# Half of a 7x7 depthwise convolution in steps between the layers of an MLP, and waits for reused memory by tile

## The chip, the cores and the metric

The kernel runs on one core of one Trainium2 chip. The metric is the device time of one execution in microseconds (us). Three executions of the kernel before took 5678.27, 5685.37 and 5686.59 us, and their median is 5685.37 us.

## What is computed

The input `x` has 8 images of 96x96 positions with 192 channels, all in float32. Two residual blocks follow one another. `_gn` is a group normalisation with 32 groups of 6 channels over a whole image.

```python
def block_0(x, W_in, b_in, conv_w, ln_g, ln_b, W_out, b_out):
    proj = einsum('bhwd,dc->bhwc', x, W_in) + b_in
    local = depthwise_conv_3x3(proj, conv_w)
    lr, rl, tb, bt = ema_scans_in_four_directions(local)
    mixed = 0.25 * (lr + rl + tb + bt) + local
    return einsum('bhwc,cd->bhwd', layer_norm(mixed) * ln_g + ln_b, W_out) + b_out

def block_1(x, dw_kernel, dw_bias, ln_gamma, ln_beta, w0, b0, w1, b1, gamma):
    y = depthwise_conv_7x7(x, dw_kernel) + dw_bias
    y = layer_norm(y) * ln_gamma + ln_beta
    y = gelu(einsum('bhwc,cd->bhwd', y, w0) + b0)
    return (einsum('bhwd,dc->bhwc', y, w1) + b1) * gamma

x = x + block_0(_gn(x), ...)
x = x + block_1(_gn(x), ...)
```

Block 0 widens 192 channels to 384, block 1 widens them to 768.

## The kernel before

The work is done in five stages, one after another, and each stores its result in device memory for the next. The order of instructions within a stage is written out by hand (`manual_schedule`); each engine works through its own list in order, and so do the lists of SP and GpSimd that issue DMAs.

1. **Projection** (to 756 us of the profiled execution). Normalised columns are turned and multiplied with `W_in`; the result goes to `P_d`.
2. **3x3 convolution and scans** (to about 1795 us). Groups of four channels are convolved by banded matrices on TensorE, scanned on VectorE (lines 631 and 640), mixed, and stored to `M_d`.
3. **Residual of block 0** (to 2639 us). A loop over 192 columns of 4 images each. Every column is loaded (`mt`, `xr`), normalised, multiplied with `wc` (line 866), added to `x` (`x1c`, line 883) and stored to `X1_d` in tiles of 16 columns (`store_c`, line 982). The statistics for the second group normalisation are taken on the way (line 903). For each half of the images a chain of six small steps turns them into a scale and a shift in `s1`. The first half's chain runs in the middle of the stage. The second half's runs at its end (lines 920 to 968), ahead of the next stage.
4. **7x7 convolution** (2680 to 3247 us). There are 32 pieces: two halves of the images (4 images each) times 16 groups of 12 channels. A piece loads `raw` from `X1_d` (six DMAs, three from SP and three from GpSimd, line 773) and its `band` of banded matrices from `Z2_d` (line 777, one DMA, SP and GpSimd by turns). VectorE copies `band` to the other 64 partitions (line 1049) and scales `raw` into `xin` (line 1059, 16 instructions). Then follow six steps of `conv_d`: 12 matmuls each of 63 rows by 64 columns (line 1079; float32 makes two records of each), on four tiles of the array, and two evictions on ScalarE (line 1089) into `yo`. Six DMAs store `yo` to `Y_d` (lines 1104 to 1109). `raw`, `band`, `xin` and `yo` have two buffers each. The loads of pieces 0 and 1 are issued in stage 3, 24 and 12 columns before its end.
5. **MLP** (3247 us to the end). There are 72 units `u` of 1024 positions, 36 in each half of the images; a block `n` of two units shares one load of `y` (from `Y_d`, line 1164) and one of `r` (from `X1_d`, line 1173). Per unit, VectorE takes statistics (`stats_e`) and normalises (`norm_e`, line 1198; its power is on GpSimd, line 29), TensorE transposes (`turn_in`, line 1213), then multiplies with `w0w` (`first_layer`, lines 1230 and 1240) in two parts of six PSUM banks. ScalarE applies Gelu (line 1249), TensorE multiplies with `w1g` in four parts `k` (`second_layer`, line 1260), VectorE adds `r` into `xo` (line 1270), and GpSimd issues the store (line 1278). GpSimd also adds the bias to `r` (`bias_r`, line 1179). First layers of unit `u` stand between second layers of unit `u - 1`. All seven banks of `hp` serve both layers; one bank serves the transposes.

Pools of tiles are opened and closed by stage. A pool that takes memory of a closed pool waits, before anything is written, until every tile of the earlier pool has been released.

## Time and profile before

| | us |
|---|---|
| median of three executions | 5685.37 |
| the profiled execution | 5683.71 |
| its span | 5681.8 |
| TensorE busy in the span (94%) | 5361.7 |
| VectorE busy (53%) | 3007.6 |
| ScalarE busy (39%) | 2226.5 |
| GpSimd busy (37%) | 2091.8 |
| second-layer matmuls, line 1260: busy | 1148.7 |
| first-layer matmuls, lines 1230 and 1240: busy | 769.3 and 409.8 |
| 7x7 matmuls, line 1079: busy | 426.5 |

By stage, TensorE is busy for 706.65 of 756 us, 1021.75 of 1039, 805.46 of 844, 435.98 of 608 (2639 to 3247 us) and 2391.90 of 2435. The DMA engines have a share of 0.86, 0.91, 0.92, 0.89 and 0.31 in these stretches.

How to read the lines shown below: PE is TensorE, PEld its weight loads, DVE VectorE, ACT ScalarE, POOL GpSimd, SP the engine that issues most DMAs. In the slices of the page each digit is the busy share of one of 40 equal parts of the span, in tenths. A table of stretches gives, for each stretch from:to, its length, the busy time of each engine with its number of instructions, the clock granted to TensorE (PEclk, 1.00 is full), the share of the 16 DMA engines that was busy, and GB/s. A line of waits names who waited for whom, the total in us, how often, and the longest. A line of DMA issues gives out<-in, the issuing queue, the number, KB each and the median us to landing.

### The profile page before, as it was taken

The page shows a single profiled execution, that of the slowest core. Times are in us where ns is not written, and L with a number is a line of the kernel's source. Part 1 is how long each engine was busy: PE and PEld are TensorE (multiplying, and loading weights), DVE is VectorE, ACT ScalarE, POOL GpSimd, SP SyncE. Part 2 cuts the span into 40 slices and gives each one's busy share as a digit, 9 for nine tenths or more (in the row PEclk, how much of TensorE's full clock was granted, in tenths as well). Part 3 has the DMA queues.
Part 4 walks back from the last instruction along what each step waited for, and adds up shares of the span by engine and source line. Part 5 has one row for each costly group of instructions (what it writes and reads, how often), then busy time and mean ns, then how long its engine had stood idle before and what let it go on. Part 6 is the DMA issues. An engine that isn't in the chain of part 4 may idle for free.

```text
span 5681.8 us, 106371 instructions
## 1 busy us (share of the span) xinstructions
PE 5361.7 (94%) x43070; PEld 3424.8 (60%) x43070; DVE 3007.6 (53%) x6098; ACT 2226.5 (39%) x5282; POOL 2091.8 (37%) x2093
## 2 busy tenths in 40 slices
PE   6999989999998999997777689999999999999999
PEld 4666633333334999986333257767777676776767
DVE  6656459999997455545444343334333333333432
ACT  2444447777775666553333322222222222222221
POOL 1111148888887555553222122222222222222221
PEclk9999989999999999998888899999999999999999
DMA  7999879999997899997999833322322332332221
GB/s 222 289 289 266 227 208 242 245 244 245 243 243 214 266 288 289 279 286 203 272 262 273 230 73 76 74 69 69 79 70 68 79 71 69 72 76 70 69 69 39
DMA packets 695475, 996.57 MB, mean 175 GB/s; under 512 B 234232, under 2 KB 576809, under 8 KB 692937
## 3 DMA queue, kind: packets, MB, share of 16 engines
q1 hardware_dynamic: 598488, 620.61, 43.6%
q0 software_dynamic: 90368, 366.55, 20.1%
q8 instruction: 340, 5.57, 0.4%
q10 hardware_dynamic: 6128, 2.61, 0.2%
q14 instruction: 151, 1.23, 0.1%
HBM read 585.22 MB, written 419.93 MB: 177 GB/s over the span
## 4 chain that ended last, share of the span: by engine, by line
PE 74%; DMA 6%; issue 3%; DVE 2%; SPq 1%; POOL 1%; ACT 0%; POOLq 0%; DVEq 0%
PE po L1260 19%; PE hp L1230 12%; PE pl L598 11%; PE po L866 10%; PE hp L1240 7%; PE pa L619 5%; PE pt L864 3%; DMA band<-Z_d 3%; DMA raw<-X_d 3%; PE pa L622 2%; PE py L1079 2%; PE pt L1213 2%; DVE xin L1059 1%; SPq L773 1%; DMA mt<-M_d 1%
## 5 line engine op out<-in xcount | busy, mean ns | idle before, releaser
L1249 ACT ACTIVATE g<-hp,b0g 128x512 f32<-128x512 f32 x864 | 514.9, 695 | 1850.3 <-PE hp L1240 1850.3
L1260 PE MATMUL po<-w1g,g 128*128 128x192 f32 x6912 | 1148.7, 326 | 0.0
L1260 PEld LDWEIGHTS po<-w1g,g 128*128 128x128 f32 x6912 | 1121.6, 190 | 1.5 <-issue 1.5
L1230 PE MATMUL hp<-yT,w0w 128*128 128x512 f32 x1728 | 769.3, 595 | 0.0
L1216 DVE COPY yT<-pt 128x512 f32<-128x512 f32 x216 | 148.8, 689 | 1058.8 <-PE pt L1213 1058.8
L866 PE MATMUL po<-wc,mt 128*128 128x193 f32 x3456 | 686.7, 334 | 2.2 <-DVE x1c L883 2.2
L598 PE MATMUL pl<-pin,band 34*32 34x380 f32 (+1 forms) x13824 | 629.3, 489 | 18.5 <-DMA pin<-P_d 18.5
L671 POOL TENSOR_TENSOR mo<-mo,z 128x768 f32<-128x768 f32 x288 | 601.4, 2089 | 3.1 <-ACT mo L623 0.2
L866 PEld LDWEIGHTS po<-wc,mt 128*128 128x128 f32 x3456 | 556.3, 192 | 32.9 <-ACT mean L868 30.1
L1079 PE MATMUL py<-xin,band 63*64 63x372 f32 (+1 forms) x4608 | 426.5, 517 | 146.6 <-DVE xin L1059 146.6
L1278 POOL DMA_DIRECT2D out_dram<-xo x288 | 210.5, 731 | 893.7 <-DVE xo L1270 876.5
L1230 PEld LDWEIGHTS hp<-yT,w0w 128*128 128x128 f32 x1728 | 322.1, 191 | 347.1 <-issue 345.4
L631 DVE TENSOR_TENSOR_SCAN z<-decay,loc 128x768 f32<-128x768 f32 x288 | 505.8, 1756 | 42.1 <-ACT loc L607 13.2
L640 DVE TENSOR_TENSOR_SCAN z<-decay,z 128x768 f32<-128x768 f32 x288 | 498.3, 1730 | 0.1
L598 PEld LDWEIGHTS pl<-pin,band 34*32 34x32 f32 x13824 | 232.3, 107 | 397.6 <-issue 395.2
L619 PE MATMUL pa<-loc,mix 128*32 128x384 f32 x3456 | 431.7, 493 | 0.0
L1270 DVE TENSOR_TENSOR xo<-po,r 128x384 f32<-128x384 f32 x288 | 232.6, 808 | 369.1 <-PE po L1260 369.1
L622 PE MATMUL pa<-last,down 96*32 96x384 f32 x1152 | 426.7, 493 | 0.9 <-ACT mo L623 0.9
L1079 PEld LDWEIGHTS py<-xin,band 63*64 63x64 f32 x4608 | 184.3, 144 | 388.3 <-issue 298.6
L1240 PE MATMUL hp<-yT,w0w 64*128 64x512 f32 x1728 | 409.8, 606 | 0.0
L29 POOL TENSOR_TENSOR rs<-rs_ve,neg_half 128x8 f32<-128x8 f32 x72 | 118.9, 1651 | 778.6 <-DVE rs_ve L28 757.5
L381 PE MATMUL pm<-xT,win 128*128 128x384 f32 x1152 | 392.2, 491 | 0.0
(133 smaller groups left out, 6693.2 us busy)
## 6 DMA issues: line engine op xcount, KB each, us to landing
P_d<-po POOLq DMA_DIRECT2D x96, 1152.0 KB, 9.9
pin<-P_d SPq DMA_DIRECT2D x192, 576.0 KB
mt<-M_d SPq DMA_DIRECT2D x192, 576.0 KB
xq<-in_x_dram SPq DMA_DIRECT2D x96, 576.0 KB
xr<-in_x_dram SPq DMA_DIRECT2D x192, 288.0 KB
X_d<-x1c SPq DMA_DIRECT2D x144, 384.0 KB
y<-Y_d SPq DMA_DIRECT2D x144, 384.0 KB
r<-X_d SPq DMA_DIRECT2D x36, 1536.0 KB
```

The lines of the kernel that those rows point to most:

```text
L598: nc.tensor.matmul(pls[g][at * RB : (at + 1) * RB, :, lo:hi], band[rows, c, kh, :], pin[rows, c, :, NJ - 1 - j, lo + kh - 1 : hi + kh - 1] ...
L619: nc.tensor.matmul(pa[at], mix[:, i, at], loc[:, q], start=True, stop=True)
L622: nc.tensor.matmul(pa[at], down[:, to], last[:, q], start=True, stop=True)
L631: nc.vector.tensor_tensor_scan(zf, decay_f, loc.rearrange("p q n -> p (q n)"), 0.0, ALU.mult, ALU.add)
L640: nc.vector.tensor_tensor_scan(zr, decay_f, zr, 0.0, ALU.mult, ALU.add)
L671: nc.gpsimd.tensor_tensor(m, m, z, ALU.add)
L866: nc.tensor.matmul(po, lhs[m], wc[:, m], start=(m == 0), stop=(m == NC - 1))
L1079: nc.tensor.matmul(pys[g][k * 64 : (k + 1) * 64, :, lo:hi], band[rows, k * GS + c, d * ZS : d * ZS + 64], xin[rows, :, :, k * GS + c, lo + ...
L1230: nc.tensor.matmul(hps[m, q], w0w[:, 2 * q, m * 128 : (m + 1) * 128], yT[:, 2 * q], start=True, stop=False,)
L1240: nc.tensor.matmul(hps[m, q], w0w[p, 1, m * 128 : (m + 1) * 128], yT[p, 1], start=False, stop=True,)
L1249: nc.scalar.activation(g[:, m, q], hps[m, q], AF.Gelu, bias=b0g[:, m : m + 1], scale=1.0)
L1260: nc.tensor.matmul(po[:, q], g[:, m, q, k * 128 : (k + 1) * 128], w1g[:, m], start=(m == 0), stop=(m == NE - 1),)
```

## The change

The change has five parts.

- **Pieces in the MLP.** Only the first 18 of the 32 pieces (`N1 = NI + 2`: all of the first half of the images and two of the second) are a stage of their own. The other 14 are cut into slots: three slots of eight scalings (the third also spreads the band) and six slots of one `conv_d` step. The loads of the next `raw` are issued with the first step; the store and the load of the next band with the last. `slot()` takes the next one, at five places of each unit of the first half's MLP.
- **First half's MLP.** The first layer runs in three parts of four banks instead of two of six. Five banks (`ps_h`) serve both layers, two (`ps_y`) the steps. In the second half the seven banks are used in turn, in two parts as before. `yn` has one buffer instead of two, and `xo` three of a quarter unit instead of two of a whole one.
- **Stage 4.** Its pieces alternate between two sets of buffers (`early` and `own`); `raw` is three tiles, one for each `t`, and 24 scalings (one for each `t`, image and group) replace 16. From piece 18 on there is one set. The band of piece `n + 1` is loaded ahead of the raw of piece `n + 2`.
- **Edges.** Piece 0 is loaded 20 columns before the end of stage 3, and scaled in its last ten. The normalisation chain of the second half stands between the steps of pieces 1 and 2. The first two `y` are loaded at piece 16, and the first unit is normalised at piece 17. `X1_d` and `Y_d` are one tensor for each half.
- **Memory.** All pools from stage 2 on have `reuse_waits="tile"`: a tile waits for the tiles that had its memory, not for the whole closed pool. `avg` moves to a pool of stage 1, `ones` is dropped.

The diff, cut to its core:

```diff
-    X1_d = dram.tile([B * ROWS + 1, NGC, NV, GC * WQ], F32, name="X1_d")
-    Y_d = dram.tile([ROWS, 2, GROUPS, NH, NV, GS * WQ], F32, name="Y_d")
+    X1_d = [
+        dram.tile([NH * ROWS + 1, NGC, NV, GC * WQ], F32, name=f"X1_{hf}") for hf in range(2)
+    ]
+    Y_d = [dram.tile([ROWS, GROUPS, NH, NV, GS * WQ], F32, name=f"Y_{hf}") for hf in range(2)]
...
+    by_tile = dict(reuse_waits="tile")
-        bp_ = ph.enter_context(tc.tile_pool(name="b_in", bufs=4))
+        bp_ = ph.enter_context(tc.tile_pool(name="b_in", bufs=4, **by_tile))
...
+    early = ctx.enter_context(tc.tile_pool(name="d_early", bufs=1, **by_tile))
+    N1 = NI + 2
+    d_pools = [early, None]
+    def load_raw(n, t):
+        hf, i = todo[n]
+        pool = d_pools[0 if n == 0 or n >= N1 else (n + 1) % 2]
+        raw = pool.tile([128, NH, NV, GC, WQ], F32, tag="raw", name="raw", bufs=NT)
...
+    def load_band(n):
+        pool = d_pools[0 if n >= N1 else n % 2]
...
+        (nc.sync, nc.gpsimd)[g].dma_start(
+            band[g * 64 : (g + 1) * 64].rearrange("q c l -> q (c l)"),
+            Z2_d[:, i * GC : (i + 1) * GC].rearrange("r c l -> r (c l)"),
+        )
+    def scale_steps(n):
...
+        for t in range(NT):
+            for b in range(NH):
+                for k in range(2):
+                    steps.append(lambda t=t, k=k, b=b: scale(t, k, b))
+        return steps + [spread]
...
-                if u in (n_u - 24, n_u - 12):
-                    first_d.append(load_d(0, len(first_d)))
+                if u == n_u - 20:
+                    load_band(0)
+                    for t in range(NT):
+                        load_raw(0, t)
+                    first_d += scale_steps(0)
+                if u >= n_u - 10:
+                    for step in first_d[:3]:
+                        step()
+                    del first_d[:3]
...
+    ps_t = ctx.enter_context(tc.tile_pool(name="e_ps_t", bufs=1, space=PSUM, **by_tile))
+    ps_h = ctx.enter_context(tc.tile_pool(name="e_ps_h", bufs=5, space=PSUM, **by_tile))
+    ps_y = ctx.enter_context(tc.tile_pool(name="d_ps", bufs=2, space=PSUM, **by_tile))
+    def bank(pool=None):
+        if pool is None:
+            pool = ps_h if ring[0] % 7 < 5 else ps_y
+            ring[0] += 1
+        return pool.tile([128, 512], F32, tag="hp", name="hp")
...
+            load_band(1)
+            for t in range(NT):
+                load_raw(1, t)
+            norms = norm_c(1, bank)
+            for n in range(N1):
+                if n:
+                    store_d(n - 1)
+                    load_band(n + 1)
+                if n == NI:
+                    load_y(0)
+                    load_y(1)
+                if n == N1 - 1:
+                    for t in range(NT):
+                        load_raw(N1, t)
+                    prepare(0)
+                else:
+                    if n + 2 < N1:
+                        for t in range(NT):
+                            load_raw(n + 2, t)
+                    for step in scale_steps(n + 1):
+                        step()
+                if n == 2:
+                    make_weights(bank())
+                for c in range(GS):
+                    conv_d(n, c)
+                    if 0 < n < 3 and c % 2:
+                        norms.pop(0)()
+            store_d(N1 - 1)
...
+        for n in range(N1, len(todo)):
+            more = n + 1 < len(todo)
+            scales = scale_steps(n)
+            slots += [scales[:8], scales[8:16], scales[16:]]
+            slots += [[lambda n=n, c=c: conv_d(n, c, ps_y)] for c in range(GS)]
+            if more:
+                slots[-GS] += [lambda n=n, t=t: load_raw(n + 1, t) for t in range(NT)]
+            slots[-1].append(lambda n=n: store_d(n))
+            if more:
+                slots[-1].append(lambda n=n: load_band(n + 1))
...
+            first_layer(u, 0, parts, pool)
+            turn_in(u + 1, 0) if u < n_u else None
+            slot()
...
+            second_layer(u - 1, 0, pool)
+            slot()
+            if early_half:
+                first_layer(u, 1, parts, pool)
+            second_layer(u - 1, 1, pool)
+            turn_in(u + 1, 1) if u < n_u else None
+            slot()
...
+            if not early_half:
+                first_layer(u, 1, parts, pool)
+            turn_in(u + 1, 2) if u < n_u else None
...
+            second_layer(u - 1, 2, pool)
+            slot()
+            if early_half:
+                first_layer(u, 2, parts, pool)
...
+            second_layer(u - 1, 3, pool)
+            slot()
```

## The prediction

> **What bounds the kernel now.** I read four views of the kernel before: the page's 40 slices, the busy time by stretch, the waits of TensorE around the 7x7 stage, and the DMA issues. The slices come first:
>
> ```profile
> PE   6999989999998999997777689999999999999999
> ...
> PEclk9999989999999999998888899999999999999999
> DMA  7999879999997899997999833322322332332221
> ```
>
> TensorE is full nearly everywhere. In slices 19 to 23, where the 7x7 convolution lies, it is not: its digit is 7 or 6, its clock is down, and DMA is at 9 in slices 20 to 22. From slice 24 on DMA falls to 2 or 3 and TensorE is full. The stretches say how much:
>
> ```profile
> core 0: us, PE busy (x) PEld busy (x) DVE busy (x) ACT busy (x) POOL busy (x), PEclk, DMA share, GB/s
> 2640.00:2700.00 60.00, 27.90 (x239) 16.76 (x243) 34.07 (x82) 7.48 (x15) 11.44 (x10) 0.63 0.51 130
> 2735.00:3247.00 512.00, 385.66 (x4172) 166.63 (x4172) 214.15 (x476) 182.07 (x347) 110.12 (x179) 0.85 0.93 258
> 3250.00:3320.00 70.00, 36.11 (x100) 15.67 (x101) 36.61 (x81) 12.01 (x19) 15.73 (x5) 0.71 0.66 131
> 3320.00:5640.00 2320.00, 2320.00 (x10940) 1639.53 (x10941) 883.74 (x2216) 500.56 (x840) 498.91 (x383) 1.00 0.30 70
> ```
>
> Pieces 3 to 32 of the convolution take 512 us, 17.07 us a piece, with the DMA engines 93% busy and TensorE only 385.66/30 = 12.86 us a piece at a clock of 0.85. The MLP pass that follows holds TensorE at 2320 of 2320 us, with DMA at 0.30, VectorE at 38%, ScalarE at 22% and GpSimd at 22%. So one stage is bound by transfers and has TensorE free, the next is bound by TensorE and has transfers free. The two stretches between stages (2640 to 2700, 3250 to 3320) are bound by neither. The waits of TensorE from 2640 to 3340 us name why:
>
> ```profile
> PE py L1079 <- DVE xin L1059: 146.6, 35, 14.1
> PE pt L1213 <- issue: 26.4, 1, 26.4
> PE gn_ps L922 <- DVE gn_ms L920: 15.8, 1, 15.8
> PE pt L1213 <- DVE yn L1198: 8.4, 11, 3.2
> ```
>
> The first is the DMA bound seen from TensorE (the scaling waits in turn for `raw` and `band`). The second is the first transpose of the MLP, which waits for the last piece to be stored and read back. The third is the group normalisation of the second half, which stands ahead of all pieces. What a piece moves comes from the DMA issues:
>
> ```profile
> raw<-X_d POOLq DMA_DIRECT2D x96, 384.0 KB, 13.3
> raw<-X_d SPq DMA_DIRECT2D x96, 384.0 KB
> ...
> Y_d<-yo SPq DMA_DIRECT2D x32, 810.0 KB
> Y_d<-yo POOLq DMA_DIRECT2D x32, 810.0 KB, 12.5
> ...
> band<-Z_d POOLq DMA_DIRECT2D x16, 624.0 KB, 9.8
> ```
>
> Over 32 pieces that is 6 x 384 + 624 + 2 x 810, and 4 edges of 27: 4656 KB a piece, or 279 GB/s at 17.07 us.
>
> **What the Trainium skill says.** "DMA: Bandwidth & Descriptors", section "Issuing engines are not separate DMA queues": transfers from all issuing engines share the same 16 DMA engines. The trace agrees: pieces issued from SP and GpSimd together reach a share of 0.93 and no more. So no reordering shortens the part that stays a stage of its own. "TensorE: Matmul & The Clock Gate", Part 3, "The mechanism": matmuls on separate tiles of the array run at once. The trace agrees: a step of 24 records of 63x64, four tiles at a time, repeats every 1.89 us at full clock (the evictions of the second piece start at 2715.21, 2717.10 and 2719.00 us), though one record lasts 473 ns. "ScalarE: Activation LUTs", "Table sets: the hidden batching unit": identity is in every set. The trace has one 1.28 us table load at the first Gelu and shows no Identity after it. I take the page's word: the convolution's evictions among the Gelus need no reload. The order of the changed program has one load there too.
>
> **The change part by part.** The sum is made in the profiled execution (span 5681.8, its own time 5683.71 us, 1.7 below the median 5685.37).
>
> *Before the convolution.* The two load bursts at the end of the residual stage each leave TensorE waiting over 7 us for `mt` (2537 to 2544 and 2597 to 2604 us; 26.5 us in three waits over the whole stage). One whole burst and half of a second remain: I take 5 us less (between 0 and 9). VectorE gets 25 more instructions there, some 9 us over ten columns of 4.1 us in which it is about half busy: nothing. The waits by tile could help the two other stage starts, where TensorE waits 18.5 us for `pin` and 9.7 + 11.9 us for `wc` and `mt`. But `pin` and the first `mt` wait for stores of data that they read, so I take 0 (between 10 gained and 3 lost, as instructions may come earlier on a busy VectorE).
>
> *Eighteen pieces as a stage.* Before, from the last residual matmul (2638.8) to the last piece (3247.2) are 608.4 us. After, piece 0 is scaled beforehand and starts at once, and the group norm moves beside pieces 1 and 2. But the last 12 stores of `x1c` (384 KB each, 4608 KB, 17 us at 279 GB/s) are still on the way. The order of the changed program shows that the load of `band` 1 on GpSimd's queue waits for them, with three `raw` loads behind it. I price that wait at 0, since DMA is full with those stores. If it were not, it would cost up to 17 us. Then 17 pieces at 17.07 = 290. The last piece's data is there before its store is, so its lag of 1.5 (band) + 6.2 (scaling) + 12.9 (matmuls) = 20.6 less a store of 1728/4656 x 17.07 = 6.3 is added: 17 + 290 + 14 = **321 us**. At a share of 1.00 instead of 0.93 it would be 20 less. With the same loss again it would be 20 more. The smaller scaling instruction (192 columns) has no row. It lies between 0.39 us x 192/288 = 0.26 and 0.45 us (the 128x192 `yn`), so 24 cost 6.2 to 10.8 a piece; both fit in 17.07.
>
> *The join to the MLP.* Before, TensorE waits 26.4 + 8.4 + 2.4 = 37 us. After, the rows of the first half are complete two pieces before the stage ends: a store lands in 12 us, `y` (4 x 384 KB) takes about 6, statistics and normalisation 5.0 + 1.7 + 2.9, against about 26 us of two pieces. Then the second unit must be normalised. `bias_r`, which stood for 5.4 us before its power on GpSimd, now comes after it. I leave 15 us (0 to 37).
>
> *Fourteen pieces in the MLP.* 84 steps of 1.89 us, and a change of tile shape in and out. In the MLP the 96 + 48 + 12 matmuls of a unit of some 33 us exceed their streaming time by about 1.1 us over eight changes of shape, 0.14 each. So I take 2.1 a step (between 1.9 and 2.6): **176 us** (160 to 218), all on the path. Three parts of the first layer instead of two: 36 units x 0.2 = 7 us. Beside it: 14 x 4656 KB over some 26 units of 39 us are 66 GB/s more, a DMA share near 0.55. ScalarE gets 12 x 0.58 us a piece, VectorE 8 to 12 us a piece of about 70 us, with room at 22% and 38%. Without that cover the pieces' transfers would cost 17.07 each.
>
> *Queues.* In each piece SP and GpSimd issue 3 `raw` loads and 3 stores; `band` alternates. On GpSimd that is 3 x 0.68 + 1.75 + 0.27 = 4 us. A store waits for ScalarE's last eviction; queued behind it are the `out` stores and the power for the next normalisation. VectorE waits for that power, then TensorE's transposes do. The store is issued in the step's own slot, so the wait should be about 2 us, and the norm has the rest of a unit: 0. The band load is issued after a piece's last step and needed three slots (some 20 us) later, against 9.8 us to land: 0. If late, about 5 us a piece, 70 in all.
>
> *Sum.* 2638.8 - 5 + 321 + (2434.6 - 37 + 15 + 176 + 7, where 2434.6 = 5681.8 - 3247.2) = 5550; with 1.9 around the span and 1.7 to the median, **5554 us**, 131 less (2.3%).
>
> **The rivals.** *Late feeding:* queues or landing hold each of the 14 pieces for 5 us: 5624. For it: on SP and GpSimd waits stand in one line with MLP traffic, and `xin`, `yo` and `band` have one buffer each here. Against: slots are some 7 us apart. *Cheaper than priced:* steps cost 1.9 (-17), the stage reaches a share of 1.0 (-20), the join is hidden (-7 more): 5510. Against it stands that the stage has kept its 0.93. *Bank wait, slower:* the steps have only two PSUM banks; their evictions queue on ScalarE behind the four Gelus of a part (4 x 0.695 = 2.8 us), and TensorE stands that long at each step: 84 x 2.8 = 235, 5789. It decides when a step exceeds 2.1 + 131/84 = 3.7 us. Against it: between two steps lie at least 24 second-layer matmuls (4 us), and ScalarE is 22% busy. *It doesn't do what it says* is excluded: the order of the changed program shows the steps between the layers on TensorE.
>
> **How the numbers follow.** Forecast 60%, cheaper 17%, late feeding 15%, bank wait 8%, a quarter of that near the point where it cancels. About 0.2% (11 us) is what a measurement of this kernel can tell from no change. Faster 0.92, same 0.02, slower 0.06. The range adds the bounds: step +42, join +22 and half of late feeding reach 5615; the cheaper case and 5 from the stage starts give 5505. Outside remain the bank wait and some of late feeding.
>
> **What would show it.** Right: the stage of 18 pieces ends some 320 us after the residual stage at a share still near 0.93; the MLP's first half has units of about 39 to 40 us with TensorE full and DMA near 0.55; steps of 2.1 us; a second half at 33 us a unit. Wrong: TensorE waits on `xin`, `band` or `yo` within the MLP, units over 43 us in its first half, or a first stage slower than 17 us a piece.

## The result, and the profile after

The changed kernel takes 5666.35 us (median of 20 runs, 5652.81 to 5688.87) against 5685.4 us for the kernel before (median of 20, 5670.99 to 5696.95). The ratio is 0.997 with a 95% interval of [0.996, 0.998]: 19 us faster, where 131 were forecast. The time lies above the range of 5505 to 5615. The profiled execution has a span of 5652.9 us and its own time of 5654.68 us; the sum of the prediction made its span 5550.4 us.

First the slices of the page, those of the prediction's first fence:

```profile
PE   5999989999998999997688999999999999999999
...
PEclk9999989999999999999789999999999999999999
DMA  7999869999997899999898456555332222322321
```

The shape is the one forecast. The stretch where TensorE is below 9 has shrunk to slices 19 to 22, though the last two are 8, not 9. DMA now stays at 4 to 6 beside a full TensorE from slice 23 to 28, where the 14 pieces are dealt out, and falls to 3 and 2 only then. Two stretches of the MLP, its first and its second half (columns as in the prediction: each engine's busy time, TensorE's clock, DMA's share, GB/s):

```profile
3050.00:4400.00 1350.00, 1327.38 (x7252) 854.78 (x7244) 582.26 (x1416) 332.46 (x571) 301.28 (x272) 1.00 0.48 107
4470.00:5653.00 1183.00, 1175.35 (x5566) 834.81 (x5564) 435.17 (x1081) 250.73 (x420) 252.87 (x197) 1.00 0.28 68
```

The loads of the convolution do run beside the MLP (a share of 0.48 against 0.28), and TensorE is busy for 1327 of 1350 us. So the saving is made. What takes it back has to be looked for stage by stage. The next table cuts both executions at the same events: the last residual matmul, the end of the last piece that runs as a stage, and the start of units 0 and 36 of the MLP.

| stretch (us) | before | forecast | after | after less forecast |
|---|---|---|---|---|
| start to the last residual matmul | 2638.8 | 2633.8 | 2649.4 | +15.6 |
| pieces as a stage (32, then 18) | 608.4 | 321 | 353.8 | +32.8 |
| from there to unit 36 (join, first half) | 1223.5 | 1384.5 | 1437.1 | +52.6 |
| unit 36 to the end of the span | 1211.1 | 1211.1 | 1212.6 | +1.5 |
| span | 5681.8 | 5550.4 | 5652.9 | +102.5 |

The forecast of the third line is 1223.5 - 37 + 15 + 176 + 7. Three stretches carry the miss, and each has its view.

**The first half of the MLP.** The table of units (start of one first layer to the next) shows units 26 to 35, which have no convolution left in them, at 34.79 us, while units 36 to 70 take 33.07 as before. Units with four steps of the convolution take 42.6 to 43.1. The waits of TensorE over these 36 units give one part of the 1.72 us:

```profile
PE pt L1226 <- DVE yT L1229: 20.1, 19, 1.2
```

It is the largest wait there, 19 times 1.06 us: `turn_in(u + 1, 1)` and `turn_in(u + 1, 2)` now stand next to each other at TensorE, and `ps_t` has one bank, so the second waits until VectorE has copied the first away. Only 19 of the 36 units pay this. In the other 17 a step of the convolution stands between the two turns, and the copy is done by the time it ends.

**The stage of 18 pieces.** The waits of TensorE from the residual's end to the first layer:

```profile
PE hp L1131 <- DVE band L817: 50.2, 8, 30.1
PE hp L1131 <- DMA band<-Z_d: 35.7, 6, 8.5
PE hp L1131 <- DVE b0g L748: 9.3, 1, 9.3
PE pt L1226 <- DVE yn L1209: 7.6, 4, 6.9
```

The longest wait, 30.1 us, lies between piece 0 and piece 1. A wait of 9.3 us is for the making of the weights. The stretches of 20 us say what the DMA engines did in that time (the residual ends at 2649.4; a share can come out a little over 1, because a packet is counted whole in the stretch in which it starts):

```profile
core 0: us, PE busy (x) PEld busy (x) DVE busy (x) ACT busy (x) POOL busy (x), PEclk, DMA share, GB/s
2639.40:2659.40 20.00, 17.23 (x128) 12.80 (x130) 13.43 (x35) 8.41 (x28) 6.46 (x6) 0.91 0.45 128
2659.40:2679.40 20.00, 6.84 (x86) 3.52 (x78) 5.05 (x15) 4.56 (x9) 4.98 (x8) 0.79 0.88 248
2679.40:2699.40 20.00, 3.07 (x20) 2.03 (x24) 11.90 (x36) 0.00 (x0) 3.72 (x5) 0.50 1.03 245
2699.40:2719.40 20.00, 17.55 (x146) 9.24 (x138) 10.74 (x29) 6.32 (x12) 5.67 (x2) 0.77 0.36 92
2719.40:2739.40 20.00, 10.69 (x94) 5.55 (x97) 9.59 (x29) 3.16 (x6) 3.97 (x7) 0.74 1.00 223
2739.40:2759.40 20.00, 19.68 (x222) 9.19 (x214) 8.40 (x28) 8.69 (x17) 3.78 (x6) 0.91 0.55 128
2759.40:3004.40 245.00, 188.09 (x2016) 114.28 (x2016) 114.78 (x331) 89.32 (x171) 58.07 (x88) 0.87 1.01 269
```

From 110 us after the residual on, DMA is full (1.01). Before that it is not: 0.45, 0.36 and 0.55 in three of six stretches leave 11 + 13 + 9 = 33 us unused. That is the size of the +32.8 of the table, but the two are not the same sum: half of the first stretch lies before the stage, and the forecast was made at a share of 0.93.

**The first stage.** It ends at 766.9 us instead of 753.8. One wait on VectorE and one on TensorE were not there before:

```profile
DVE blk L914 <- DMA Z_d<-z: 9.8, 1, 9.8
```

```profile
PE pm L381 <- DVE po L405: 8.0, 1, 8.0
```

The constants `blk` and `pick` of the group norm have a pool of their own now and wait by tile, so their first write rises to 95.2 us, into the first stage. There it waits for a transfer, the evictions of the first stage stand behind it, and TensorE stands behind those. The wait is 8.0 of the 13.1 us. After it TensorE's clock is down as well (0.53 from 90 to 100 us, where `e4_blk`, which is told of below, has 1.00), and in this execution its first matmul comes 2.4 us later than in the one before (43.1 against 40.7 us).

### The profile page after: what moved, and what is told of

Same layout as the page of the kernel before. It is cut to its first block, busy times and chain, and to the rows that moved or that the text cites. A ratio compares the mean times of both kernels' runs of the same rounds, so it can differ in the third digit from the quotient of the medians.

```text
span 5652.9 us, 106714 instructions
## 1 busy us (share of the span) xinstructions
PE 5393.8 (95%) x43070; PEld 3443.0 (61%) x43070; DVE 3066.6 (54%) x6353; ACT 2233.1 (40%) x5282; POOL 2103.9 (37%) x2093
## 4 chain that ended last, share of the span: by engine, by line
PE 77%; DMA 4%; issue 2%; DVE 2%; POOL 1%; SPq 0%; ACT 0%; POOLq 0%; DVEq 0%; ACTq 0%
PE hp L1274 19%; PE hp L1244 13%; PE pl L599 11%; PE po L981 11%; PE hp L1254 7%; PE pa L620 5%; PE hp L1131 4%; PE pt L979 3%; PE pa L623 2%; PE pt L1226 2%; DMA raw<-X 1%; DMA band<-Z_d 1%; DVE xin L806 1%; DMA Y<-yo 1%; DMA mt<-M_d 0%
## 5 line engine op out<-in xcount | busy, mean ns | idle before, releaser
L1274 PE MATMUL hp<-w1g,g 128*128 128x192 f32 x6912 | 1170.8, 328 | 4.0 <-DVE xo L1285 4.0
L1274 PEld LDWEIGHTS hp<-w1g,g 128*128 128x128 f32 x6912 | 1121.2, 190 | 68.6 <-issue 42.5
L1285 DVE TENSOR_TENSOR xo<-hp,r 128x384 f32<-128x384 f32 x288 | 230.6, 801 | 739.3 <-PE hp L1274 739.3
L981 PEld LDWEIGHTS po<-wc,mt 128*128 128x128 f32 x3456 | 554.8, 191 | 32.3 <-ACT mean L983 30.1
L1131 PE MATMUL hp<-xin,band 63*64 63x372 f32 (+1 forms) x4608 | 430.0, 509 | 101.2 <-DVE band L817 51.8
L1141 ACT ACTIVATE yo<-hp,dwb 128x384 f32<-128x384 f32 x384 | 202.2, 578 | 608.2 <-PE hp L1131 443.2
L1131 PEld LDWEIGHTS hp<-xin,band 63*64 63x64 f32 x4608 | 211.6, 141 | 278.7 <-issue 244.7
```

The source lines that it names most:

```text
L981: nc.tensor.matmul(po, lhs[m], wc[:, m], start=(m == 0), stop=(m == NC - 1))
L1131: nc.tensor.matmul(pys[g][k * 64 : (k + 1) * 64, :, lo:hi], band[rows, k * GS + c, d * ZS : d * ZS + 64], xin[rows, :, :, k * GS + c, lo + ...
L1274: nc.tensor.matmul(po[:, q], g[:, m, q, k * 128 : (k + 1) * 128], w1g[:, m], start=(m == 0), stop=(m == NE - 1),)
```

## The experiments

Each one changes the kernel after the change, except where it says otherwise. The table collects the time and the same cuts (profiled execution; "to unit 0" is from the last residual matmul to the first first-layer matmul).

| kernel | median us | stage 1 ends | last residual | to unit 0 | units 0 to 35 | units without steps |
|---|---|---|---|---|---|---|
| before | 5685.4 | 753.8 | 2638.8 | 640.4 | 1191.5 | 33.07 |
| after | 5666.35 | 766.9 | 2649.4 | 366.9 | 1424.0 | 34.79 |
| e2_parts | 5638.51 | 765.9 | 2661.3 | 380.6 | 1393.9 | 33.07 |
| e1_turn | 5645.28 | 764.8 | 2660.7 | 376.5 | 1409.9 | 33.51 |
| e5_own | 5664.43 | 766.1 | 2645.2 | 367.1 | 1433.6 | 34.79 |
| e4_blk | 5655.37 | 754.9 | 2635.1 | 380.4 | 1427.1 | 34.79 |
| e6_later | 5669.12 | 764.7 | 2663.8 | 377.5 | 1430.0 | 34.79 |
| e8_own_later | 5674.84 | 765.2 | 2661.6 | 372.6 | 1425.6 | 34.79 |
| e7_all | 5613.44 | 755.0 | 2634.4 | 372.2 | 1393.0 | 33.07 |
| b1_tile | 5683.96 | 754.6 | 2642.2 | 638.0 | 1192.2 | 33.07 |
| c1_nonorm | 5615.5 | 755.3 | 2635.5 | 354.7 | 1430.1 | 34.79 |
| c2_first | 5648.12 | 755.3 | 2635.1 | 365.1 | 1433.7 | 34.79 |
| c3_best | 5613.96 | 755.3 | 2635.6 | 374.0 | 1393.7 | 33.07 |
| c4_ahead | 5601.31 | 756.1 | 2633.7 | 359.8 | 1393.8 | 33.07 |

"To unit 0" varies by 13 us between kernels that are alike in that stretch (after and e4_blk), through the pace of the later pieces (17.2 to 17.8 us) and the join. A difference below that is not read from one profile. The profiled execution is not the median one either: it took 5650.16 us in `e2_parts`, 5661.53 in `e1_turn`, 5685.65 in `e6_later` and 5634.63 in `c1_nonorm`. Gains are therefore read from the medians, and places from the cuts.

### The order in three parts

`e2_parts`: two parts in the first half too, all seven banks in turn for layers and steps.

```diff
-            parts, pool = (3, ps_h) if early_half else (2, None)
+            parts, pool = 2, None
...
+            early_half = False
...
-            slots += [[lambda n=n, c=c: conv_d(n, c, ps_y)] for c in range(GS)]
+            slots += [[lambda n=n, c=c: conv_d(n, c)] for c in range(GS)]
```

> The MLP of the first half goes in two parts, as that of the second half does, and its matmuls and the steps take all seven banks in turn; nothing else of the change is touched. Theory 1 (the order in three parts costs 1.7 us in each of the 36 units, because tile shapes change more often and because the second and third turn of the input stand back to back on one bank): units 26 to 35, which have no steps, fall from 34.8 us to 33.07, the first half from 1424 us to about 1370, and the time by about 55 us, to 5600 to 5615. Rival (what slows these units is the loads and stores of the convolution, or the weights and tables of the second half, which run beside them): units 26 to 35 stay at 34.5 us or more and the time within 10 us of 5666. Second rival (the three parts keep steps and layers out of each other's banks, and are worth their price): units without steps fall to 33.07, but a step goes from 2.06 us to 2.7 or more, since it waits for a bank, and the time stays or grows.

Measured: 5638.51 us, ratio to before 0.9908 [0.9891, 0.9926], so 28 us below the changed kernel. Units 26 to 35 take 33.07 us: the excess was the order in three parts, and not the transfers beside them, which are the same. The rival of the transfers falls. But the first half shrinks by 30 us and not by 55. The expectation charged 1.72 us to all 36 units, and the wait between the turns comes in 19. With the parts that `e1_turn` gives below (1.28 and 0.44 us a unit), the three parts cost 19 x 1.28 + 36 x 0.44 = 40 us. About 10 of these are lost again here, most of them in other waits of TensorE in these units: 17.1 us (6.7 for the copy of `band`, 5.7 and 4.7 once each) against 9.3 in the changed kernel. The second rival falls too: from its first matmul to the next instruction a step takes 2.06 us (median) in both kernels. What a unit grows by is more than that, 2.28 us a step ((42.18 - 33.07)/4), and the same with three parts once no turn waits ((42.62 - 33.51)/4 in `e1_turn`).

`e1_turn`: only the third turn moves.

```diff
-            turn_in(u + 1, 2) if u < n_u else None
+            if not early_half:
+                turn_in(u + 1, 2) if u < n_u else None
...
             second_layer(u - 1, 2, pool)
+            if early_half:
+                turn_in(u + 1, 2) if u < n_u else None
             slot()
```

> Only the third turn of the next unit's input is moved behind the second layer of the last part, so that the second and third turn no longer stand next to each other; the order in three parts stays. Theory 1a (the back-to-back turns on one bank are 1.05 us of the 1.72): units 26 to 35 fall from 34.8 to about 33.7 us, the wait of the turn for the copy on VectorE is gone from the waits, and the time falls by 10 to 30 us, since units whose slot between the turns has a step lose nothing now. Rival (the change of shape itself is the cost, not the wait): the wait is gone but units stay at 34.5 us or more, time unchanged within 5 us.

Measured: 5645.28 us, ratio 0.9933 [0.9921, 0.9945], 21 us below the changed kernel. Units without steps take 33.51 us, the wait on VectorE's copy falls from 20.1 to 0.8 us. So of the 1.72 us a unit, 1.28 belong to the two turns side by side, and 0.44 remain for the shorter groups: in the changed kernel the first layer's matmuls start to start take 3 x (3.53 + 1.91) = 16.3 us a unit, in two parts 2 x (5.24 + 2.78) = 16.0. The starts show 0.28 of the 0.44. The forecast's 0.2 us a unit was meant for this second part and is half of it. It had no term for the first.

### The constants in the first stage

`e4_blk`: the writes of `blk` and `pick` go to the thirteenth unit of the third stage's loop.

```diff
-        nc.vector.memset(blk, 0.0)
-        for b in range(NH):
...
+                if u == 12:
+                    nc.vector.memset(blk, 0.0)
+                    for b in range(NH):
...
```

> The small constants of the group norm are written inside the third stage's loop at its thirteenth unit, not ahead of it. Theory 1 (with waits by tile these writes rose into the first stage, where VectorE stands 9.8 us behind a transfer and TensorE 8.0 us behind VectorE): that wait is gone, the first stage ends near 758 us, not 766, and the time falls by 6 to 13 us. Rival (the 13 us that the first stage grew by come from elsewhere, the wait is only where it shows): the first stage still ends at 763 us or later; time within 4 us of 5666.

Measured: 5655.37 us, ratio 0.9942 [0.9929, 0.9954], 11 us below the changed kernel. The first stage ends at 754.9, and the last residual matmul comes at 2635.1: 1.3 us from the forecast's 2633.8. The rival falls: the writes of the constants are what makes the first stage longer.

`b1_tile` asks whether waits by tile alone do this. It is the kernel before with `reuse_waits="tile"` on every pool from the second stage on.

> The kernel before, with waits by tile on all pools from the second stage on and nothing else changed. Theory 1 (waits by tile gain some us at the third stage, 8 to 11 by the two traces, and lose as much in the first, where the constants rise into it): time within 8 us of 5685, the first stage 8 to 13 us longer, the third stage's passes shorter. Rival (the changes of stages 1 to 3 are run to run scatter or come from the order of the convolution): stage boundaries as in the kernel before, within 4 us. Second rival (waits by tile are a gain of 10 us or more in all): 5675 or less.

Measured: 5683.96 us, ratio 1.0002 [0.9993, 1.001]. The first stage ends at 754.6, the third stage's passes take 819.8 us against 817.3. Theory 1 falls, the first rival stands: waits by tile do nothing measurable to the kernel before. So waits by tile alone do not let the constants rise; they did so together with the new pool, and whether the new pool alone would do it was not run. The third stage's passes are 10 us shorter in the changed kernel (807.2 us): TensorE has one wait of over 7 us for `mt` left in them, where it had two. Since waits by tile do not do this, the new order of the convolution's loads is what remains; it was not tested on its own.

### The start of the stage of 18 pieces

`e5_own`: the tiles `yo` and `xin` of piece 1 are allocated first in `own`, so that `band` 1 does not lie on memory that the stores of `x1c` still read.

```diff
             d_pools[1] = own
+            yos[1] = own.tile([128, NB, NH * NV, GS, WQ], F32, tag="yo", name="yo")
+            xins[1] = own.tile([128, NT, NH, GC, WV], F32, tag="xin", name="xin")
             load_band(1)
```

> The two big tiles of piece 1 are allocated first in their pool, so that the band of piece 1 comes to lie on memory that the stores of the last passes do not read. Theory 1 (TensorE's 30 us of idle time behind conv piece 0 is the band of piece 1, whose DMA waits 21 us on GpSimd for the stores because it reuses memory that they read): the wait on GpSimd is gone, TensorE's wait for the band falls from 30 us to under 10, the stage of 18 pieces from 353 us to 325 to 335, and the time by 15 to 28 us. Rival (the DMA engines are full at this point anyway, 0.70 to 1.05 busy, so that the band lands as late whoever issues it): the wait on GpSimd is gone, but the band lands within 5 us of before and the stage stays at 345 to 355 us; time within 8 us of 5666.

Measured: 5664.43 us, ratio 0.9966 [0.9952, 0.9979]: no difference. The timelines of GpSimd, of SP's queue and of VectorE (start, duration, the wait in brackets), first of the changed kernel:

```profile
2672.90 0.57 POOL L790 DMA_DIRECT2D band<-Z_d  x1 [21.40 <-DMA Y<-yo]
```

```profile
2652.10 13.37 SPq L1034 DMA_DIRECT2D X<-x1c  x12
```

```profile
2687.33 7.37 DVE L806 TENSOR_SCALAR xin<-raw,s 128x192 f32<-128x192 f32 x24 [22.88 <-DMA raw<-X]
```

and the same three lines of `e5_own`:

```profile
2649.93 0.57 POOL L790 DMA_DIRECT2D band<-Z_d  x1 [2.67 <-issue]
```

```profile
2647.87 27.25 SPq L1034 DMA_DIRECT2D X<-x1c  x12
```

```profile
2680.29 7.31 DVE L806 TENSOR_SCALAR xin<-raw,s 128x192 f32<-128x192 f32 x24 [20.07 <-DMA raw<-X]
```

GpSimd's wait of 21.4 us is gone, and its loads start 19 us earlier (4.7 us after the residual instead of 23.5). But the twelve stores now take 27.25 us to issue, not 13.37, and the scaling of piece 1 starts 35.1 us after the residual instead of 37.9. The rival holds: the engines are full with the same bytes, and the order of issue changes little. The step of the prediction that priced this wait at 0 was right.

`e6_later`: the norm at pieces 4 and 5, the weights at piece 8.

```diff
-                if n == 2:
+                if n == 8:
                     make_weights(bank())
...
-                    if 0 < n < 3 and c % 2:
+                    if 3 < n < 6 and c % 2:
```

> The group norm's chain is spread over pieces 4 and 5 instead of 1 and 2, and the making of the last layer's weights goes to piece 8 instead of 2; nothing else is touched. Theory 1 (the stage of 18 pieces is bound by DMA, and the 33 us that it is longer than forecast are DMA idle time in its first 110 us, part of it because the next loads wait for scales that stand on VectorE behind the norm chain and for convs that stand on TensorE behind the weights): DMA's share between 50 and 110 us after the residual rises from about 0.65 to 0.85 or more, piece 4 starts 95 to 108 us after the residual instead of 115 to 119, and the stage and the time shrink by 8 to 20 us. Rival (the fill is set by the stores of the last passes and the first loads alone, the norm only lies in their shade): piece 4 starts at 112 us or later, time within 5 us of 5666.

Measured: 5669.12 us, ratio 0.9974 [0.9958, 0.999]. DMA's share from 50 to 110 us after the residual rose to 0.69, 1.03 and 1.01, and piece 4 starts at 99 us, both as theory 1 had it. The time did not fall. TensorE's waits for the norm grew from 2.5 to 26 us (15.7 for `gn_rb`, 10.3 for `gn_ms`), and DMA's share is 0.43 from 110 to 130 us and 0.55 from 150 to 170. The hole moves with the norm. So it is the norm that makes it, and not the place at the start of the stage.

`e8_own_later` joins the two edits.

> The order of the norm and the weights as in the run above, and with it the tiles of piece 1 allocated first, as in the run on its own that brought 2 us. Theory 1 (holes in the DMA's work add up, and each early load that can be issued fills one): 3 to 8 us below the run with the order alone. Rival (the early load only shares the engines with the stores that it no longer waits for): the same as the run with the order alone, within 3 us.

Measured: 5674.84 us, ratio 0.9988 [0.998, 0.9997]. No gain: the rival again (5.7 us above `e6_later`, where the two kernels scatter over 28 and 30 us).

`c1_nonorm`, with the constants as in `e4_blk`, leaves norm and weights out.

```diff
-            norms = norm_c(1, bank)
+            nc.vector.tensor_copy(s1[:, 1], s1[:, 0])
...
-                if n == 2:
-                    make_weights(bank())
...
-                    if 0 < n < 3 and c % 2:
-                        norms.pop(0)()
```

> With the constants written inside the third stage (5655 us on its own), the group norm's chain of the second half and the making of the last layer's weights are left out: the second half takes the scales and shifts of the first, and the last layers' weights stay unscaled, so that part of the computation is missing. It prices what norm and weights cost in the stage of 18 pieces, wherever they stand. Theory 1 (they make a hole in the DMA's work, early or later): the stage up to the first layer falls from 367 to 380 us to 345 to 358, the time to 5630 to 5645. Rival (the 33 us come from the fill alone: piece 1 stands behind the stores of the last passes and no load can run ahead for want of buffers): piece 1 still starts at 44 us or later after the residual, the stage falls by less than 8 us, time at 5647 or more.

Measured: 5615.5 us, ratio 0.9894 [0.9875, 0.9913], 40 us below `e4_blk` by the medians; the stage up to the first layer is 354.7 us, 12 below the changed kernel's and 26 below `e4_blk`'s. Piece 4 starts at 98 us instead of 118. The stretches from 50 to 110 us after the residual:

```profile
2685.50:2705.50 20.00, 20.00 (x240) 13.57 (x236) 12.97 (x40) 10.10 (x20) 4.38 (x7) 0.93 0.65 156
2705.50:2725.50 20.00, 11.37 (x112) 7.65 (x108) 6.27 (x17) 4.63 (x9) 4.19 (x6) 0.74 1.03 284
2725.50:2745.50 20.00, 17.11 (x190) 9.79 (x184) 11.04 (x33) 8.10 (x16) 5.24 (x7) 0.91 1.02 268
```

The shares are 0.65, 1.03 and 1.02, where the changed kernel has 0.36, 1.00 and 0.55: 15 of the 22 unused microseconds are gone. Piece 1 still starts at 47.4 us. So norm and weights cost about 20 us in this stage, and the start of piece 1 is another matter. The 20 us are read from the stage and not from the medians: two of the five times are 5634.6 us, the profiled one among them, and three 5613 to 5616, and what parts them was not found.

`c2_first`, with the constants as in `e4_blk` and the tiles as in `e5_own`, loads the raw data of piece 1 ahead of the last stores.

```diff
+            for t in range(NT):
+                load_raw(1, t)
             for store in stores:
                 store()
...
             load_band(1)
-            for t in range(NT):
-                load_raw(1, t)
```

> With the constants written inside the third stage (5655 us on its own), the raw data of piece 1 are loaded ahead of the last 12 stores of the residual stage, not behind them, and the tiles of piece 1 are allocated first; the norm stays at pieces 1 and 2. Theory of the fill (piece 1 starts 47 us after the residual, not at 17, since its loads share the DMA engines with 4608 KB of stores that nobody needs yet): raw data of piece 1 land 12 to 20 us earlier, piece 1 starts 25 to 35 us after the residual, DMA's share in the 10 us around the residual's end rises from 0.46 to 0.8 or more, time 5637 to 5648. Rival (the whole of what has to be moved before piece 2 is the same, so the gain is given back at pieces 2 to 4): piece 1 starts earlier, but piece 4 still at 110 us or later, and the time within 5 us of 5655.

Measured: 5648.12 us, ratio 0.9939 [0.9926, 0.9952], 7 us below `e4_blk`. Piece 1 starts at 43.9 us, piece 4 at 115. The theory of the fill falls in this form: the scaling of piece 1 now waits 19.9 us for the stores themselves, since `xin` 1 lies on the memory of `x1c`. In this layout the memory that piece 1 needs is free only when the stores are done, whatever is issued first.

Why do norm and weights make a hole, when their instructions keep VectorE busy for only some 9 us? VectorE's timeline in the changed kernel shows it for the weights:

```profile
2717.47 7.15 DVE L806 TENSOR_SCALAR xin<-raw,s 128x192 f32<-128x192 f32 x24 [3.82 <-PE hp L1131]
2734.99 1.45 DVE L817 COPY band<-band 64x2496 f32<-64x2496 f32 x1 [10.37 <-DMA band<-Z_d]
...
2738.36 0.16 DVE L748 TENSOR_TENSOR b0g<-b0g,hp 128x6 f32<-128x6 f32 x1
```

The 24 scales of the next piece come first, then the copy of its band, which waits 10.37 us for the transfer, and only then the weights' arithmetic. At TensorE the product for `b0g` already holds a bank, and the 9.3 us wait shown above is its. In this stage, which is fed just in time, whatever stands behind the next piece's scales on VectorE waits for the next piece's data. The steps of the norm go back and forth between TensorE and VectorE, so each of the two stands for the other in the middle of a piece. `c4_ahead` tests this on the kernel with all useful edits. Two steps lead up to it.

`e7_all` first: two parts, constants, tiles, norm later.

> Four edits at once: two parts in the first half, the constants inside the third stage, the tiles of piece 1 first, the norm and the weights later. If the causes are apart in time, as all theories hold, the gains add: 28 for the parts, 11 for the constants, 2 for the tiles, and what the order brings (0 to 20): 5605 to 5625 us. If one of them hid another, 5630 or more.

Measured: 5613.44 us, ratio 0.9877 [0.9864, 0.9891]. That is 53 us below the changed kernel, in the range expected, but more than the single edits sum to (28 + 11 + 2 - 3 = 38). A part of the rest may be the second stage, which is 3 us shorter than in the changed kernel's profile and 17 to 19 shorter than in those of `e2_parts` and `e6_later` (see the last section).

`c3_best`: norm and weights back at pieces 1 and 2, the early raw load in.

> Two parts in the first half, constants in the third stage, tiles of piece 1 first and its raw data ahead of the last stores; the norm at pieces 1 and 2 as in the changed kernel. The kernel with four edits, where the norm was later, took 5613. If the late norm gave nothing and the early load gives what its theory says: 5595 to 5608. If the early load gives nothing: 5610 to 5618.

Measured: 5613.96 us, ratio 0.9877 [0.9859, 0.9896]: the same.

`c4_ahead` differs from it in this alone:

```diff
+                    if n == 3:
+                        make_weights(bank())
+                    if 3 < n < 10:
+                        norms.pop(0)()
                     for step in scale_steps(n + 1):
                         step()
-                if n == 2:
-                    make_weights(bank())
...
-                    if 0 < n < 3 and c % 2:
-                        norms.pop(0)()
```

> As the kernel with two parts, constants in the third stage and the early raw load (5614 us), but the six steps of the group norm are put ahead of the scales of the next piece, one step per piece at pieces 4 to 9, and the weights ahead of the scales at piece 3. Theory 1 (norm and weights cost some 20 us because on VectorE they stand behind the scales of the next piece, which wait for its raw data, while TensorE stands in the middle of a conv for their result; ahead of the scales nothing waits): TensorE's waits for the norm and the weights are gone, DMA's share from 50 to 110 us after the residual is 0.85 or more, piece 4 starts near 98 us as in the run without them, the stage up to the first layer is 12 to 22 us shorter, time 5593 to 5602. Rival (norm and weights cost TensorE's and VectorE's own time wherever they stand): the stage shrinks by less than 6 us, time 5609 to 5617.

Measured: 5601.31 us, ratio 0.9851 [0.9835, 0.9867], 13 us below `c3_best`, with the stage 14 us shorter (359.8 against 374.0). In `c3_best` TensorE waits 9.5 us for `b0g`, and VectorE 8.0 us for the norm's products on TensorE (4.3, 3.1 and 0.6):

```profile
PE hp L1134 <- DVE b0g L748: 9.5, 1, 9.5
```

```profile
DVE s L893 <- PE hp L884: 4.3, 1, 4.3
DVE gn_ve L870 <- PE hp L866: 3.1, 1, 3.1
```

Both are gone in `c4_ahead`. What is left are two waits of TensorE ahead of a piece:

```profile
PE hp L847 <- DVE gn_ms L845: 5.9, 1, 5.9
...
PE hp L866 <- DVE gn_ds L864: 1.2, 1, 1.2
```

Piece 4 starts at 97.8 us, as in the run without norm and weights, and the DMA stretches from 50 to 110 us are

```profile
2683.70:2703.70 20.00, 20.00 (x248) 13.65 (x240) 9.70 (x29) 11.57 (x22) 4.38 (x7) 1.00 0.67 148
2703.70:2723.70 20.00, 15.78 (x150) 11.50 (x153) 11.30 (x34) 4.78 (x11) 4.18 (x6) 0.74 1.03 302
2723.70:2743.70 20.00, 14.11 (x149) 6.42 (x145) 11.39 (x32) 5.99 (x13) 5.09 (x7) 0.83 1.02 263
```

Theory 1 holds: the work itself costs little, and where it stands costs the rest. With norm and weights the stage is now 5 us longer than without them (359.8 against 354.7 in `c1_nonorm`), instead of some 20. But the edit does three things at once. It puts the steps ahead of the scales, takes them out of the middle of a piece, and spreads the norm over pieces 4 to 9. Later pieces alone gave nothing (`e7_all` has the norm at pieces 4 and 5 and takes the same time as `c3_best`). Which share the order has and which the spreading was not separated. At 5601.31 us it is the fastest kernel of this study, 65 us below the changed one and 84 below the one before.

## Why the prediction was wrong, point by point

The mechanism was right: the transfers of 14 pieces hide beside the MLP, nothing in it waits for them to speak of (TensorE's waits for `band` and `xin` over 36 units are 3.0 us), and no step waits for a bank. What failed are four terms of the sum, each in the direction of more time. The two largest are the start of the 18 pieces and the order in three parts.

- *"Eighteen pieces as a stage: 321 us."* Measured 353.8. The pace came out as forecast (17.2 us a piece from piece 4 on, against 17.07), but by luck. The 17.07 divides 512 us by 30 pieces, and the line shown has 4172 matmul records of 144 a piece: 29 pieces, 17.66 us each. At that pace the forecast would have been 10 us longer. The pieces then ran 0.4 us faster than before. The term "17" for the stores and the first piece was too small: piece 4 starts 118 us after the residual, where 17 + 4 x 17.07 = 85 were forecast. In the kernel before, with the whole norm ahead of its pieces, the fifth one started after 111 us: the head start bought nothing. About 20 us of the 33 are the norm and the weights, which the prediction moved "beside pieces 1 and 2" at no price (`c1_nonorm`: 118 to 98; `c4_ahead`: the same with the work still done, by its place and spacing). The remaining 13 are the start of piece 1, 47 us after the residual where 17 + 17.07 = 34 were forecast. The DMA engines idle half of the 20 us around the residual's end. `c2_first` shows that memory is in the way (19.9 us of waiting for the stores), and did not remove the 13 us. That free memory would remove them was not tried. The prediction also said that no reordering shortens this stage; `c4_ahead` shortens it by 14 us with the same transfers.
- *"Three parts of the first layer instead of two: 36 units x 0.2 = 7 us."* Measured about 40 us. The two turns of the input side by side on one bank are 1.28 us in each of 19 units (`e1_turn`); the new order shows them and the prediction did not look for them. The shorter groups are 0.44 us in all 36, where 0.2 was taken.
- *"So I take 2.1 a step ... 176 us."* A unit grows by 2.28 us a step, 191 us for 84, within the stated bounds. The 0.14 us for a change of shape was too small, and it does not follow from the trace: inside their groups the matmuls of a unit start 0.16, 0.43 and 0.11 us apart, which makes some 32.4 of the 33.07 us and leaves 0.7 for eight changes, not 1.1.
- *"The waits by tile could help the two other stage starts ... I take 0 (between 10 gained and 3 lost)."* The constants rose into the first stage and cost it some 12 us (`e4_blk`: 754.9 instead of 766.9). The sign was wrong: a memset of 0.17 us stood 9.8 us for a transfer, with the evictions behind it. The reason given in the same sentence ("instructions may come earlier") was the right one to follow up, but it was asked of the second and third stage's starts alone.

Right were: the join (unit 0 starts 13 us after the last piece, 15 forecast), the wait for `band` 1 on GpSimd (0), the queues in the MLP (0), the 24 scalings of a piece (7.1 to 7.4 us, between 6.2 and 10.8), and the second half at 33.07 us. The 168 Identity evictions among the Gelus brought no table load: the trace has two in all, as before. The -5 for the end of the residual stage was right only in the total: the third stage gained 5.6 us, because its passes are 10 us shorter and its start is 4.5 us longer. The sum of the misses: 13.1 for the first stage and 3.1 for the second, less 0.6 for the third; 32.8 for the 18 pieces; 33 for the three parts and 15 for the steps, beyond what was priced; some 6 for other waits in these units, less 2 at the join; and 1.5 in the second half. That makes 102, of 102.5 in the spans. The 12 us from the profiled execution (5654.68) to the median are the scatter of this kernel, which is told of below.

Of the signs named beforehand, two showed themselves: the 18 pieces as a stage take 353.8/18 = 19.7 us each, where the 321 us meant 17.8, and the units with convolution take 41.6 us on average, not 39 to 40. The range was also narrower than its own bounds: 5554 + 42 + 22 is 5618 already, and half of the late feeding makes it 5653, not 5615.

Of the rivals, late feeding and the bank wait of the steps did not occur (second-layer products waited twice for a bank, 2.0 us each). "Cheaper than priced" did not either. Its premise came true in part, for the share was 1.01 over the last 245 us of the stage, but a piece took 17.2 us there against 17.66 before: 7 us over 17 pieces, not 20. None of the rivals was about the start of a stage, a queue on VectorE or two turns on one bank, and there most of the time went.

## What to carry to other kernels

When small work is moved beside a stage that is fed just in time, price its place in each engine's queue and not its duration: behind the next tile's work it waited for the next tile's data and cost this stage some 20 us; ahead of it, and spread over more pieces, it cost 5. When a stage is split, its start is paid in full for fewer pieces, so cost the start from the first events of the stage before (here its fifth piece had started after 111 us, though its norm stood ahead of all pieces) and not from its steady pace. And when an order is changed to separate banks, look in the new order for two users of a one-bank pool that have become neighbours, and count in how many units they really are. A pace is best divided out of the records that a stretch holds, not out of the number of pieces that one expects in it.

## What was not expected of the hardware

TensorE's clock at the start of the second stage. The stretches of the kernel before, then of the changed one, then of `e2_parts`:

```profile
790.00:800.00 10.00, 10.00 (x176) 3.29 (x176) 8.42 (x5) 6.79 (x17) 4.57 (x4) 0.92 0.92 191
```

```profile
800.00:810.00 10.00, 10.00 (x102) 2.59 (x90) 6.34 (x4) 3.70 (x9) 2.51 (x3) 0.50 0.88 190
810.00:820.00 10.00, 10.00 (x181) 3.42 (x180) 8.81 (x6) 6.75 (x17) 4.65 (x5) 0.96 0.85 189
```

```profile
820.00:830.00 10.00, 10.00 (x100) 2.52 (x88) 4.09 (x3) 4.00 (x10) 2.60 (x3) 0.50 0.25 51
830.00:840.00 10.00, 10.00 (x128) 2.79 (x124) 6.12 (x4) 4.25 (x11) 4.32 (x4) 0.66 0.37 80
```

TensorE is busy throughout each of them. In the kernel before, its clock (the third number from the end) is back at full speed from about 791 us, in the changed kernel from 811, in `e2_parts` from about 837. The Trainium skill, "TensorE: Matmul & The Clock Gate", Part 1, "What's actually happening", gives about 3.4 us of sustained work for the return to full clock. This case's traces differ, and they decide: the convs of the second stage run on without a gap from 773.8 us in the kernel before, 786.9 in the changed one and 786.0 in `e2_parts`, so it was 18, 24 and 51 us. In the profiles, the second stage (from the end of the first to its own last matmul) takes 1040.7 to 1041.7 us in all eight kernels whose constants are not in the first stage (before and `b1_tile` among them) and in `e5_own`, but 1044.4 in the changed kernel and 1057.1 to 1059.6 in `e2_parts`, `e1_turn`, `e6_later` and `e8_own_later`. The longer the clock is down, the longer the stage: by the clock records it is at 0.50 for 34.1 us in these eight and `e5_own`, 41.0 in the changed kernel, and 68.3 to 75.1 in the last four. All that show the longer stage have the wait in the first stage, but `e5_own` has it too and does not. The length of the waits for `pin` is not the reason, since `e4_blk` has the same (9.5 and 9.1 us, in `e2_parts` 9.5 and 9.2). The times agree with this in part: the changed kernel scatters over 36 us in 20 runs, `e4_blk`, `e7_all`, `c2_first` and `c3_best` over 5.5 to 6.8 in 4 to 6 runs each, but `c4_ahead` over 11, `b1_tile` over 17 in 13 runs, `c1_nonorm` over 21, and the kernel before over 26. How a wait of 8 us that ends at 96 us goes with a low clock some 700 us later was not found.
